# Key and value projections of six blocks of self attention: seven half-size products in place of eight, combined where they are stored

## Chip, cores and metric

The kernel runs on one core of one Trainium2 chip. The metric is device time in microseconds (us) of one execution. Before the change it is 2795.85 us, the median of 3 runs (2795.35 to 2799.18).

## What is computed

An encoder over a short context (2 x 77 tokens) and one decoder layer over 2 x 2048 tokens of width D = 512, 16 heads of 32, all in float32. The change concerns the keys and values of the decoder's causal self attention:

```python
yn = _ln(y, dec_n1_s, dec_n1_b)
wq, wk, wv = jnp.split(w_in, 3, axis=0)          # 512 x 512 each
bq, bk, bv = jnp.split(b_in, 3, axis=0)
q = yn @ wq.T + bq;  k = yn @ wk.T + bk;  v = yn @ wv.T + bv      # 16 heads of 32
scores = q k^T / sqrt(32) + bias            # relative bias, causal
attn = softmax(scores);  o = attn v
y = y + o @ w_out.T + b_out
```

After it come cross attention to the encoded context and a feed forward part of width 2048.

## The kernel before, in words

**Blocks, units and slots.** The tokens of each of the two sequences (b) are cut into 4 blocks (m) of MB = 512 tokens. A block is worked off in 16 units: 4 groups g of 4 heads times 4 tiles t of 128 queries, g outermost. So there are 128 units, numbered n; block x = 4b + m starts at unit u = 16x. A unit scores its queries against all keys up to its own, in pieces of up to four key tiles of 128, takes the exponential on ScalarE (ACT), turns the probabilities on TensorE (PE, line 425), copies them out of psum on ACT and VectorE (DVE; lines 429 and 431) and multiplies them by the values (line 442). The scores (line 374) of four heads run on four row groups of PE and go to four psum banks, which DVE empties with a running maximum (lines 383 and 390; line 400 closes the unit). Psum banks are handed out in rotation among 7.

**Slots.** Between the pieces of the units other work is put into numbered slots, one per unit, in an order written out by hand: `light[n]` first, then the `jobs[n]`, then `late[n]`; `ahead[n]` runs shortly before slot n. All engines have their instructions in this one program order, each engine goes through its own in order, and SyncE (SP) issues all loads and stores from one queue.

**Projections.** Each job of the list is a load and a run. `q_job` and `k_job` (lines 212 to 234) load 128 of the 512 output features (256 KB) into one of two `wqk` buffers and make one product of 4 accumulated matmuls of 128x128 weights by 512 tokens; a query tile is scaled on DVE (line 218), a key tile goes straight into `kT` with its bias, on DVE for m of 2 and 3 (line 230), else on ACT (line 232). `v_job` (lines 236 to 245) takes 128 tokens as the stationary operand and all of the 512x512 value weights as the moving one; they are loaded as 1 MB into `wbig` for each block, which `out_job` needs for the output weights in between. Line 243 adds the bias row `bv` on DVE into `vv`. A float32 matmul is two instructions on PE in the profile. A block of m = 1 to 3 has its key and value products in the slots -4 to 6 around its start u, one product to a slot or two. `load_next` keeps loads at most three jobs ahead and at most two of the `wqk` kind.

**Around it.** Slots also hold the layer norm of the next block (loads of x at slot +5 to +8 of the block before, statistics on DVE, centering on GpSimd (POOL, line 294), turning at PE line 306 and ACT line 311 one slot later), the reciprocal sums that go through DRAM (`rec` stores at line 463, `rirows` loads at line 468, four of each per group, and the product on POOL at line 470), the loads of the bias tables (line 342, four of 128 KB), and in the first 29 slots the encoder (weights of 1 MB each, line 521; its softmax steps on POOL at lines 594 and 606). In the blocks with m = 2, sums of weights for the feed forward part are made on POOL (line 1113, helper `minus`) and stored: that later part already uses seven half-size products for each eight, from line 1376 on. In the blocks of b = 1 the cross attention of the very first block is done beside self attention.

Of the kernel before, what the change touches and what calls it, by code (L numbers as in the profile page):

```python
# [12 lines left out]
ALU = mybir.AluOpType  # L13
# [41 lines left out]
def tile_encoder_decoder(ctx: ExitStack, tc: tile.TileContext, ins, out):  # L55
# [103 lines left out]
    with (  # L159
# [40 lines left out]
            nc.sync.dma_start(w, wchunk(name, c0, P))  # L200
            return w

        def big_w(kind, b, m):
            if wbig.get("is") != (kind, b, m):
                w = wbt
                nc.sync.dma_start(
                    w, wchunk("dec_sa_in_wT", 2 * D) if kind == "v" else wchunk("dec_sa_out_wT", 0)
                )
                wbig["is"], wbig["w"] = (kind, b, m), w
            return wbig["w"]  # L210

        def q_job(b, m, g):
            def run(w):
                mm = bank()
                for c in range(NC):
                    nc.tensor.matmul(mm, w[:, c, :], nTs[b, m][:, c, :], start=(c == 0), stop=(c == NC - 1))
# [19 lines left out]
        def v_job(b, m, t):  # L236
            def run(w):
                mm = bank()
                for c in range(NC):
                    nc.tensor.matmul(  # L240
                        mm, nTs[b, m][:, c, ts(t, P)], w[:, c, :], start=(c == 0), stop=(c == NC - 1)
                    )
                nc.vector.tensor_tensor(vv[:, m * TB + t, :], mm, bv, ALU.add)

            return lambda: big_w("v", b, m), run, False

        def out_job(b, m, t):
            def run(w):
                x1 = xr.pop((b, m, t))
                mm = bank()  # L250
                for c in range(NC):
                    nc.tensor.matmul(  # L252
                        mm, ots[b, m, c][:, ts(t, P)], w[:, c, :], start=(c == 0), stop=(c == NC - 1)
                    )
                nc.vector.tensor_tensor(x1, mm, x1, ALU.add)
                nc.sync.dma_start(y1[b][m][:, t, :], x1)

            return lambda: big_w("o", b, m), run, False

        def residual_load(b, m, t, place=None):  # L260
            x1 = sb.tile([P, D], F32, name="xr", tag="xr", bufs=2) if place is None else place
# [663 lines left out]
            return plan  # L925


        blocks = [(b, m) for b in range(B) for m in range(NMB)]
        NU = NC * TB
        jobs = {n: [] for n in range(-1, len(units) + NU)}  # L930
# [5 lines left out]
        for x, (b, m) in enumerate(blocks):  # L936
            u = x * NU
            first = m == 0

            jobs[max(u - 5 + (x == 1), -1)].append(q_job(b, m, 0))  # L940
            jobs[max(u - 4 + (x == 1), -1)].append(k_job(b, m, 0))
            jobs[(u + 1 if first else u - 3 + (x == 1)) if x else -1].append(v_job(b, m, 0))
            jobs[(u + 2 if first else u - 2 + (x == 1)) if x else 1].append(v_job(b, m, 1))
            jobs[u + 3 if first else u + 1].append(v_job(b, m, 2))
            jobs[u + 4 if first else u + 2].append(v_job(b, m, 3))
            jobs[u - 1 if x else 0].append(q_job(b, m, 1))
            jobs[u if x else 2].append(k_job(b, m, 1))
            for g, at, then in ((2, 3, 4), (3, 5, 6)) if x else ((2, 6, 7), (3, 8, 9)):
                jobs[u + at].append(q_job(b, m, g))
                jobs[u + then].append(k_job(b, m, g))  # L950
# [76 lines left out]
        light[-1].append(lambda: row_into(bo, "dec_sa_out_b"))  # L1027
        light[0].append(lambda: [self_bias(relg, vg, g) for g in range(1, NC)])
        light[1].append(lambda: make_bias(0, rel, v))
        light[6].append(lambda: make_bias(2, rel, v))  # L1030
        def slot(n):
            for f in light[n]:
# [59 lines left out]
        light[len(units) - 1].append(last_loads)  # L1092


        TOK = MB // 2
        gp, ve = nc.gpsimd, nc.vector


        w1_d = dram.tile([4, NC, P, D], F32, name="w1_d")
# [12 lines left out]
        def minus(engine, out, a, b):  # L1112
            engine.tensor_tensor(out, a, b, ALU.subtract)  # L1113

        def w2_sums(c):

# [49 lines left out]
        def quarter(name, r, c):  # L1166

            return ins[name][r * TOK : (r + 1) * TOK, c * TOK : (c + 1) * TOK].rearrange("(c p) o -> p c o", p=P)

        def wc_sums(name, turned):  # L1170
            z = free.rearrange("p (z k o) -> p z k o", z=8, k=2)
            q = {}
            for i, (r, c) in enumerate(((0, 0), (0, 1), (1, 0), (1, 1))):
                nc.sync.dma_start(z[:, i], quarter(name, c, r) if turned else quarter(name, r, c))
                q[r, c] = z[:, i]
            s1, s2, s3, s4 = (z[:, 4 + i] for i in range(4))
            if turned:
                gp.tensor_tensor(s1, q[1, 0], q[1, 1], ALU.add)
                minus(gp, s2, s1, q[0, 0])
                minus(gp, s3, q[0, 0], q[1, 0])  # L1180
                minus(gp, s4, q[0, 1], s2)
            else:
                minus(gp, s1, q[0, 1], q[0, 0])
                minus(gp, s3, q[1, 1], q[0, 1])
                minus(gp, s2, q[1, 1], s1)
                minus(gp, s4, q[1, 0], s2)

        def wc_store(dst):
            nc.sync.dma_start(
                dst.rearrange("s p x -> p s x"), free[:, 4 * D :].rearrange("p (s x) -> p s x", s=4)  # L1190
            )

        for u, name, turned, dst in (
            (2 * NU, "dec_ca_in_wT", True, wq_d), (6 * NU, "dec_ca_out_wT", False, wo_d)
        ):
            light[u + 7].append(lambda name=name, turned=turned: wc_sums(name, turned))
            late[u + 8].append(lambda dst=dst: wc_store(dst))
# [95 lines left out]
        def of_n(name):  # L1293
# [5 lines left out]
        T_OF = {"T1": ("12", "11"), "T2": ("22", "T1"), "T3": ("22", "12"), "T4": ("21", "T2")}  # L1299

        def sum_n(name, of):
            minus(gp, of(name), *(of(a) for a in T_OF[name]))


        sets = [[high[:, (4 * a + k) * D : (4 * a + k + 1) * D] for k in range(4)] for a in range(2)]
# [397 lines left out]
```

## Time and profile before

| | |
|---|---|
| median of 3 runs | 2795.85 us |
| profiled execution | 2796.27 us |
| its span, first to last instruction | 2794.2 us |
| mean granted clock of TensorE | 0.997 |
| self attention stage | about 0 to 1760 us of the span |
| DMA, mean over the span | 127 GB/s |

The page gives for each engine the time that it was busy, its share of the span and the number of instructions. PE is matmuls, PEld the loading of their weights, which overlaps. Groups of instructions are named by line and operation, with output <- input, shape and count, then busy time and mean ns of one, then the idle time of the engine just before them and what ended it. The timeline lists instructions in order, merged when alike: start, length, engine, line. Rows of waits give engine and line, what it waited for, the sum in us, how often, and the longest.

### The profile page before, as it was taken

The numbers are of one execution on the slowest core, as the hardware profiler recorded it, in microseconds if no ns is written. First come the engines' busy times: TensorE is split into PE (matmuls) and PEld (weight loads), VectorE is DVE, ScalarE is ACT, GpSimd is POOL, SyncE is SP. The second block draws the span as 40 slices with busy tenths as digits, with TensorE's granted clock in tenths as the row PEclk, the third lists the DMA queues.
The fourth block names the chain that finished last, engine by engine and source line by source line (L and its number), as shares of the span: only waits on it lengthen the run. The fifth ranks groups of instructions, "written<-read, shape, count | busy, mean of one in ns | idle before, by whom it ended". The sixth has DMA issues, their size and how long they took to land. (4 is left out here: it accounts for less than half of the span.)

```text
span 2794.2 us, 65938 instructions
## 1 busy us (share of the span) xinstructions
PE 2764.6 (99%) x25998; PEld 2076.6 (74%) x25998; DVE 1858.0 (66%) x5360; ACT 1435.3 (51%) x2751; POOL 875.6 (31%) x745
## 2 busy tenths in 40 slices
PE   9999999999999999999999999999999999999998
PEld 5567666666666556666666667898989898989898
DVE  5666587778887577687778885565555656464645
ACT  3544466656666556666646666434344444444431
POOL 0301143300100312122200001364747474746456
PEclk9999999999999999999999999999999999999999
DMA  6414344411112512232311014574747565656475
GB/s 194 116 56 135 111 143 123 139 31 48 38 41 73 140 47 70 84 107 92 106 33 39 26 50 134 174 242 145 237 152 236 175 226 163 223 162 220 148 226 181
DMA packets 281271, 355.31 MB, mean 127 GB/s; under 512 B 37968, under 2 KB 156544, under 8 KB 280834
## 3 DMA queue, kind: packets, MB, share of 16 engines
q1 hardware_dynamic: 280962, 351.10, 40.6%
q8 instruction: 206, 3.38, 0.5%
q14 instruction: 103, 0.84, 0.1%
HBM read 309.51 MB, written 41.49 MB: 126 GB/s over the span
## 5 line engine op out<-in xcount | busy, mean ns | idle before, releaser
L405 ACT ACTIVATE pp<-pp,nm 128x128 f32<-128x128 f32 (+15 forms) x512 | 612.0, 1203 | 137.2 <-DVE nm L400 136.8
L383 DVE TENSOR_SCALAR_CACHE_REDUCE pp<-psum 128x512 f32<-128x512 f32 (+3 forms) x1024 | 559.5, 591 | 64.0 <-PE psum L374 62.0
L431 ACT COPY pts<-psum 128x512 f32<-128x512 f32 (+3 forms) x592 | 300.5, 577 | 505.6 <-PE psum L425 369.7
L425 PEld LDWEIGHTS psum<-ident,pp 128*128 128x128 f32 x4352 | 473.1, 141 | 107.8 <-DVE pp L383 51.6
L425 PE MATMUL psum<-ident,pp 128*128 128x128 f32 x4352 | 533.6, 277 | 8.4 <-ACT pp L405 2.9
L429 DVE COPY pts<-psum 128x512 f32<-128x512 f32 (+2 forms) x544 | 330.0, 660 | 69.2 <-PE psum L425 67.7
L374 PE MATMUL psum<-kT,q 32*128 32x512 f32 (+3 forms) x2560 | 355.7, 576 | 5.2 <-DVE pp L383 2.6
L442 PEld LDWEIGHTS psum<-pts,vv 128*32 128x32 f32 x8704 | 225.6, 110 | 123.7 <-issue 115.8
L1405 PE MATMUL psum<-pp 128*128 128x128 f32 x2560 | 304.5, 276 | 1.9 <-POOL pp L1113 1.6
L1405 PEld LDWEIGHTS psum<-pp 128*128 128x128 f32 x2560 | 296.3, 192 | 8.6 <-issue 2.8
L442 PE MATMUL psum<-pts,vv 128*32 128x128 f32 x8704 | 278.2, 275 | 0.7 <-ACT pts L431 0.5
L1113 POOL TENSOR_TENSOR pp<-pp 128x512 f32<-128x512 f32 x159 | 212.5, 1353 | 111.1 <-DMA pp<-in_dec_ff_wT_dram 52.0
L1376 PE MATMUL psum<-vv,pp 128*128 128x256 f32 x1024 | 236.2, 381 | 0.0
L374 PEld LDWEIGHTS psum<-kT,q 32*128 32x128 f32 x2560 | 123.2, 183 | 140.7 <-issue 91.2
L1376 PEld LDWEIGHTS psum<-vv,pp 128*128 128x128 f32 x1024 | 190.3, 190 | 25.8 <-issue 0.5
L390 DVE CUSTOM_DVE_ANT_0 pp<-psum,bias 128x256 f32<-128x256 f32 (+1 forms) x512 | 196.0, 411 | 15.3 <-PE psum L374 15.2
L1389 DVE TENSOR_TENSOR kT<-kT,psum 128x512 f32<-128x512 f32 x96 | 65.8, 686 | 190.7 <-PE psum L1376 190.5
L1376 PE MATMUL psum<-nT,pp 128*128 128x256 f32 x768 | 174.1, 380 | 0.0
L1392 ACT ACTIVATE kT<-kT,vecs 128x256 f32<-128x256 f32 x192 | 87.0, 501 | 156.7 <-DVE kT L1389 156.0
L287 POOL TENSOR_TENSOR rstd<-rstd,mhalf 128x1 f32<-128x1 f32 x32 | 18.5, 578 | 458.7 <-DVE rstd L286 378.6
L1376 PEld LDWEIGHTS psum<-nT,pp 128*128 128x128 f32 x768 | 144.2, 190 | 20.3 <-issue 1.6
L470 POOL TENSOR_TENSOR oT<-rirows,oT 128x512 f32<-128x512 f32 x30 | 38.6, 1287 | 363.8 <-DMA rirows<-rec 187.8
(211 smaller groups left out, 3784.8 us busy)
## 6 DMA issues: line engine op xcount, KB each, us to landing
pp<-w_d SPq DMA_DIRECT2D x520, 256.0 KB
pp<-in_dec_ff_wT_dram SPq DMA_DIRECT2D x112, 256.0 KB
wqk<-in_dec_sa_in_wT_dram SPq DMA_DIRECT2D x64, 256.0 KB
bias<-tzg SPq DMA_DIRECT2D x128, 128.0 KB
pp<-wo_d SPq DMA_DIRECT2D x56, 256.0 KB
wbig<-in_dec_sa_in_wT_dram SPq DMA_DIRECT2D x8, 1024.0 KB
vv<-in_enc_ff_wT_dram SPq DMA_DIRECT2D x8, 1024.0 KB
xr<-in_x_dram SPq DMA_DIRECT2D x32, 256.0 KB
```

The lines of the kernel that those rows point to most:

```text
L374: nc.tensor.matmul(banks[r][:, : kn * P], q[rows4(r), ts(t, P)], kT[rows4(r), g, k0 * P : (k0 + kn) * P], start=True, stop=True,)
L383: nc.vector.tensor_scalar(p[:, k0 * P : (k0 + far) * P], s[:, : far * P], 1.0, None, ALU.mult, ALU.max, accum_out=st["mx"][:, r, c : c + 1],)
L390: nc.vector.tensor_tensor_reduce(p[:, (i + 1) * P - w : (i + 1) * P], s[:, far * P : kn * P], biases[b, m, g][:, r, 2 * P - w :], 1.0, LOW ...
L405: nc.scalar.activation(p, p, AF.Exp, bias=nm, accum_out=to)
L425: nc.tensor.transpose(pt[:, ts(x, P)], state[n]["p"][r][:, ts(k, P)], ident)
L429: nc.vector.tensor_copy(pts[:, : len(load), :], pt[:, :w])
L431: nc.scalar.copy(pts[:, : len(load), :], pt[:, :w])
L442: nc.tensor.matmul(ot[rows4(r), t, :], vv[:, k, ts(g * HC + r, HD)], got.pop((n, k, r)), start=(k == 0), stop=(k == i),)
L1113: engine.tensor_tensor(out, a, b, ALU.subtract)
L1376: nc.tensor.matmul(mm[:, ts(f, TOK)], a[:, c, ts(f, P)], b[:, c, :], start=fresh and f == 0 and c == 0, stop=c == 1, skip_group_check=True,)
L1392: nc.scalar.activation(dst[:, e, :], src[:, e, :], AF.Relu, bias=vec("dec_ff1_b", f + e))
L1405: nc.tensor.matmul(psum[:, bank_i, ts(col, P)], lhs[:, c, :], w[:, c, :], start=fresh and k in (0, 3) and c == 0, stop=c == 3, skip_group_ ...
```

## The change

For the six blocks with m of 1 to 3 the key and the value projection become seven products of half size each, by Strassen's scheme in Winograd's form. The weights (512 features in, 512 out) and the normalized tokens (512 features by 512 tokens) are both cut into quarters of 256x256. Four sums of weight quarters, S1 to S4, are made once for keys and once for values on POOL in the slots 2 and 5 (`wc_sums`, in a free part of `kT`) and kept in DRAM (`wc_store`, one slot later). Four sums of token quarters, T1 to T4, are made on POOL for each block five slots before it starts (`token_sums`), in the `xt` and `xr` buffers. Each product (`part_job`) loads 256 KB of weights into a `wqk` buffer, runs 2 x 2 matmuls with 256 columns into one psum bank, and is added on DVE into one or two quarters of `kT` or `vv`; the first one of seven is copied by ACT (keys with the bias of the first half of the features; `kstep`, the difference to that of the second half, is added with product 7).

The value bias is left out of `vv` in all blocks. Since the probabilities sum to one it can go to the output row: `fold_job` multiplies it by the output weights in slot 21 (one product of 512 columns, line 1048 of the changed program) and adds it to `bo`. The `wbig` buffer is reloaded only when its kind changes, no longer for each block. The order of products and slots, relative to u:

```diff
-            jobs[max(u - 5 + (x == 1), -1)].append(q_job(b, m, 0))
-            jobs[max(u - 4 + (x == 1), -1)].append(k_job(b, m, 0))
-            jobs[(u + 1 if first else u - 3 + (x == 1)) if x else -1].append(v_job(b, m, 0))
...
+            if first:
...
+            else:
+                (late if x == 1 else light)[u - 5].append(lambda b=b, m=m: token_sums(b, m))
+                todo = {
+                    -5: "q0", -4: "k1 k6", -3: "k7 k4", -2: "k2 k5", -1: "k3 v1", 0: "v6 v7", 1: "v4 v2", 2: "q1",
+                    3: "v5 v3", 4: "q2", 5: "q3",
+                } if x > 1 else {
+                    -4: "q0 k1", -3: "k6 k7", -2: "k4 k2", -1: "k5 k3", 0: "v1 v6", 1: "v7 v4 v2", 2: "q1",
+                    3: "v5 v3", 4: "q2", 5: "q3",
+                }
...
+            if x == 0:
+                jobs[NU + 5].append(fold_job())
```

Where the products go and what they are made of:

```diff
+        T_OF = {"T1": ("12", "11"), "T2": ("22", "T1"), "T3": ("22", "12"), "T4": ("21", "T2")}
+        PARTS = {
+            1: ("11", "11"), 2: ("12", "21"), 3: ("S4", "22"), 4: ("22", "T4"),
+            5: ("S1", "T1"), 6: ("S2", "T2"), 7: ("S3", "T3"),
+        }
+        ADDS = {2: ("11",), 3: ("12",), 5: ("22", "12")}
...
+            def run(w):
+                n, mm = of_nT(b, m, by), bank()
+                left, right = (w, n) if kind == "k" else (n, w)
+                for f in range(2):
+                    for c in range(2):
+                        nc.tensor.matmul(
+                            mm[:, ts(f, TOK)], left[:, c, ts(f, P)], right[:, c, :], start=c == 0, stop=c == 1,
+                        )
+                got = mm.rearrange("p (f n) -> p f n", f=2)
...
+                elif i == 6:
+                    ve.tensor_tensor(d["12"], got, d["11"], ALU.add)
...
+                else:
+                    for to in ADDS[i]:
+                        ve.tensor_tensor(d[to], got, d[to], ALU.add)
```

The rest of the diff in its core:

```diff
-            if wbig.get("is") != (kind, b, m):
+            if wbig.get("is") != kind:
...
-                nc.vector.tensor_tensor(vv[:, m * TB + t, :], mm, bv, ALU.add)
+                nc.vector.tensor_copy(vv[:, m * TB + t, :], mm)
...
-                row_into(bv, "sa_bv")
...
+        for n, kind in ((2, "k"), (5, "v")):
+            light[n].append(lambda kind=kind: wc_sums("dec_sa_in_wT", True, spare, sa_from[kind]))
+            late[n + 1].append(lambda kind=kind: wc_store(sa_d[kind], spare))
```

The helpers for such sums move up in the file from the feed forward part, and the store of four sums there becomes four stores.

More of the change, by code (lines that the diff above doesn't have):

```diff
@@ L208, in big_w @@
                 )
-                wbig["is"], wbig["w"] = (kind, b, m), w
+                wbig["is"], wbig["w"] = kind, w
             return wbig["w"]
@@ L925, in first_cross, with minus, sum_n, quarter @@
             return plan
+        TOK = MB // 2
+        gp, ve = nc.gpsimd, nc.vector
+        def minus(engine, out, a, b):
+            engine.tensor_tensor(out, a, b, ALU.subtract)
+        T_OF = {"T1": ("12", "11"), "T2": ("22", "T1"), "T3": ("22", "12"), "T4": ("21", "T2")}
+        def sum_n(name, of):
+            minus(gp, of(name), *(of(a) for a in T_OF[name]))
+        def quarter(name, r, c, c0=0):
+            o = c0 + c * TOK
+            return ins[name][r * TOK : (r + 1) * TOK, o : o + TOK].rearrange("(c p) o -> p c o", p=P)
@@ new lines, in wc_sums @@
+        def wc_sums(name, turned, z, c0=0):
+            z = [t.rearrange("p (k o) -> p k o", k=2) for t in z]
+            q = {}
+            for i, (r, c) in enumerate(((0, 0), (0, 1), (1, 0), (1, 1))):
+                nc.sync.dma_start(z[i], quarter(name, c, r, c0) if turned else quarter(name, r, c, c0))
+                q[r, c] = z[i]
+            s1, s2, s3, s4 = z[4:]
+            if turned:
+                gp.tensor_tensor(s1, q[1, 0], q[1, 1], ALU.add)
+                minus(gp, s2, s1, q[0, 0])
+                minus(gp, s3, q[0, 0], q[1, 0])
+                minus(gp, s4, q[0, 1], s2)
+            else:
+                minus(gp, s1, q[0, 1], q[0, 0])
+                minus(gp, s3, q[1, 1], q[0, 1])
+                minus(gp, s2, q[1, 1], s1)
+                minus(gp, s4, q[1, 0], s2)
@@ new lines, in wc_store @@
+        def wc_store(dst, z):
+            for i in range(4):
+                nc.sync.dma_start(dst[i], z[4 + i])
+        sa_d = {k: dram.tile([4, P, D], F32, name=f"sa_{k}", tag=f"sa_{k}") for k in "kv"}
+        sa_from = {"k": D, "v": 2 * D}
+        kstep = sm.tile([P, 2], F32, name="kstep", tag="kstep", bufs=1)
+        n_tiles = {}
+        PARTS = {
+            1: ("11", "11"), 2: ("12", "21"), 3: ("S4", "22"), 4: ("22", "T4"),
+            5: ("S1", "T1"), 6: ("S2", "T2"), 7: ("S3", "T3"),
+        }
@@ new lines, in part_job, with load, place @@
+        def part_job(kind, b, m, i):
+            name, by = PARTS[i]
+            def load():
+                w = sb.tile([P, NC, P], F32, name="wqk", tag="wqk", bufs=2).rearrange("p c o -> p (c o)")
+                w = w.rearrange("p (c o) -> p c o", c=2)
+                if name[0] == "S":
+                    src = sa_d[kind][int(name[1]) - 1].rearrange("p (c o) -> p c o", c=2)
+                else:
+                    src = quarter("dec_sa_in_wT", int(name[1]) - 1, int(name[0]) - 1, sa_from[kind])
+                nc.sync.dma_start(w, src)
+                return w
+            def place(to):
+                r, c = int(to[0]) - 1, int(to[1]) - 1
+                if kind == "k":
+                    return kT[:, 2 * r : 2 * r + 2, m * MB + c * TOK : m * MB + (c + 1) * TOK]
+                return vv[:, m * TB + 2 * c : m * TB + 2 * c + 2, ts(r, TOK)]
+            def run(w):
[7 more added lines that the diff above has]
+                got = mm.rearrange("p (f n) -> p f n", f=2)
+                d = {to: place(to) for to in ("11", "12", "21", "22")}
+                if i == 1 and kind == "k":
+                    for f in range(2):
+                        nc.scalar.activation(
+                            d["11"][:, f, :], got[:, f, :], AF.Identity, bias=vec("dec_sa_in_b", NC + f)
+                        )
+                elif i == 1:
+                    nc.scalar.copy(d["11"], got)
+                elif i == 6:
+                    ve.tensor_tensor(d["12"], got, d["11"], ALU.add)
+                elif i == 7 and kind == "k":
+                    for f in range(2):
+                        ve.scalar_tensor_tensor(
+                            d["22"][:, f, :], got[:, f, :], kstep[:, f : f + 1], d["12"][:, f, :], ALU.add, ALU.add
+                        )
+                elif i == 7:
+                    ve.tensor_tensor(d["22"], got, d["12"], ALU.add)
+                elif i == 4:
+                    ve.tensor_tensor(d["21"], got, d["22"], ALU.add)
+                else:
+                    for to in ADDS[i]:
+                        ve.tensor_tensor(d[to], got, d[to], ALU.add)
+            return load, run, True
@@ L928, in tile_encoder_decoder, with fold_job, run @@
+        def fold_job():
+            def run(w):
+                mm = bank()
+                for c in range(NC):
+                    nc.tensor.matmul(
+                        mm, vec("dec_sa_in_b", 2 * NC + c).to_broadcast([P, P]), w[:, c, :],
+                        start=(c == 0), stop=(c == NC - 1),
+                    )
+                ve.tensor_tensor(bo, mm, bo, ALU.add)
+            return lambda: big_w("o"), run, False
         blocks = [(b, m) for b in range(B) for m in range(NMB)]
@@ L1029, in tile_encoder_decoder @@
         light[1].append(lambda: make_bias(0, rel, v))
+        light[1].append(
+            lambda: minus(ve, kstep, *(vecs[:, o : o + 2] for o in (_COL["dec_sa_in_b"] + NC + 2, _COL["dec_sa_in_b"] + NC)))
+        )
+        spare = [kT[:, g, (2 + h) * MB : (3 + h) * MB] for g in range(NC) for h in range(2)]
+        for n, kind in ((2, "k"), (5, "v")):
+            light[n].append(lambda kind=kind: wc_sums("dec_sa_in_wT", True, spare, sa_from[kind]))
+            late[n + 1].append(lambda kind=kind: wc_store(sa_d[kind], spare))
         light[6].append(lambda: make_bias(2, rel, v))
@@ L1092, in tile_encoder_decoder @@
         light[len(units) - 1].append(last_loads)
-        TOK = MB // 2
-        gp, ve = nc.gpsimd, nc.vector
         w1_d = dram.tile([4, NC, P, D], F32, name="w1_d")
@@ L1110, in tile_encoder_decoder @@
         SUBS = ("11", "21", "T2", "T1", "T3", "22", "T4")
-        def minus(engine, out, a, b):
-            engine.tensor_tensor(out, a, b, ALU.subtract)
         def w2_sums(c):
@@ L1164, in w1_store @@
             )
[L1166 to L1191, printed above, removed]
         for u, name, turned, dst in (
@@ L1195, in tile_encoder_decoder @@
         ):
-            light[u + 7].append(lambda name=name, turned=turned: wc_sums(name, turned))
-            late[u + 8].append(lambda dst=dst: wc_store(dst))
+            z = free.rearrange("p (z x) -> p z x", z=8)
+            z = [z[:, i] for i in range(8)]
+            light[u + 7].append(lambda name=name, turned=turned, z=z: wc_sums(name, turned, z))
+            late[u + 8].append(lambda dst=dst, z=z: wc_store(dst, z))
         u = 2 * NU
```

42 lines of the change are left out of this document (28 added, 14 removed).

## The prediction

> **What bounds the kernel now.** I read first the page's busy shares and the 40 slices, then the windows of the self attention stage, then the PE timeline inside one unit.
>
> ```profile
> span 2794.2 us, 65938 instructions
> PE 2764.6 (99%) x25998; PEld 2076.6 (74%) x25998; DVE 1858.0 (66%) x5360; ACT 1435.3 (51%) x2751; POOL 875.6 (31%) x745
> ```
>
> ```profile
> 80.00:160.00 80.00, 73.22 (x587) 41.61 (x584) 50.16 (x192) 39.08 (x113) 24.13 (x17) 0.96 0.28 72
> 640.00:780.00 140.00, 139.93 (x1705) 95.28 (x1702) 118.84 (x370) 90.93 (x135) 16.74 (x13) 1.00 0.16 48
> 1500.00:1600.00 100.00, 99.97 (x1231) 68.07 (x1224) 82.03 (x250) 62.80 (x88) 5.09 (x4) 1.00 0.12 38
> ```
>
> The window columns are length, PE, PEld, DVE, ACT, POOL, clock, DMA share, GB/s. PE has no idle time in the deep blocks (139.93 of 140), while DVE is at 82 to 85%. A busy PE can hide stalls, so I took the pitch, start to start, from the timeline; the last two rows are of the feed forward stage, whose products have the new shape:
>
> ```profile
> 1469.85 3.60 PE L240 MATMUL psum<-wbig,nT 128*128 128x512 f32 x8
> 1473.38 1.14 PE L374 MATMUL psum<-kT,q 32*128 32x512 f32 x8
> ...
> 1870.21 7.07 PE L1376 MATMUL psum<-nT,pp 128*128 128x256 f32 x32
> 1877.12 0.60 PE L781 MATMUL psum<-ident,q 128*128 128x128 f32 x4
> ```
>
> A value product (8 instructions of 512 columns) takes 1473.38 - 1469.85 = 3.53 us of PE; 32 instructions of 256 take 6.91, so 8 take 1.73. The engine runs such groups end to end. PE's own work is the bound, except around 100 to 121 us and where its weights wait for DVE:
>
> ```profile
> PEld psum L425 <- DVE pp L383: 51.6, 83, 1.5
> ```
>
> That is 51.6 us in 83 waits, none over 1.5.
>
> **The change, part by part.** Times go against the profiled execution, 2796.27 us (span 2794.2 and 2.07 around it), 0.4 above the median of 2795.85.
>
> *PE.* In each of six blocks 4 key and 4 value products go: 8 x 3.53 = 28.2 us. 14 half-size ones come: 14 x 1.73 = 24.2. What 3.53 has over 2 x 1.73, 0.07, I read as the change to the row-tiled scores; it is paid in 7 slots, 0.5 to 0.7 in all. Saving 28.2 - 24.2 - 0.6 = 3.4 per block, 20.4 in six. fold_job adds one product of 512 columns, 3.53. Net **-16.9 us** of PE work.
>
> *DVE and ACT.* The rows that go and the nearest of those that come:
>
> ```profile
> L243 DVE TENSOR_TENSOR vv<-psum,row_sa_bv 128x512 f32<-128x512 f32 x32 | 22.1, 692 | 59.9 <-PE psum L240 59.9
> L230 DVE TENSOR_SCALAR kT<-psum,vecs 128x512 f32<-128x512 f32 x14 | 10.5, 750 | 17.1 <-PE psum L227 17.1
> L232 ACT ACTIVATE kT<-psum,vecs 128x512 f32<-128x512 f32 x16 | 10.9, 684 | 28.9 <-PE psum L227 28.8
> L390 DVE CUSTOM_DVE_ANT_0 pp<-psum,bias 128x256 f32<-128x256 f32 x432 | 169.8, 419 | 12.7 <-PE psum L374 12.7
> ```
>
> Per block 13 adds of 128x512 into the destination come (6 for keys, 7 for values) and two of 128x256: 13 x 0.692 + 2 x 0.42 = 9.8 us. Four value adds go (2.8), and four key evictions, on DVE for m of 2 and 3 (3.0), on ACT for m = 1. DVE gains 4.0 in four blocks and 7.0 in two: 30 us. ACT gains three copies of about half a microsecond per block and loses 2.7 where m = 1. If DVE were the bound this would cost 30 us; it idles 15 to 18% in the tightest windows, some 20 us per 140, so its share rises by a few per cent. What matters is the queue: behind a part's add stand the score evictions that free psum banks. Before, one add of 0.69 to 0.75 stood there; now the first part's add ends during the second part's 1.73 us of PE, so only the second part's counts, 0.69, except after k5 (two adds, 1.38). One slot per block, 0.7 later: 0 to 4 us in all, I take 0.5, since the slot's values products lie in between.
>
> *POOL.* 4 sums per block and 8 for the weights:
>
> ```profile
> L1113 POOL TENSOR_TENSOR pp<-pp 128x512 f32<-128x512 f32 x35 | 44.0, 1275 | 52.8 <-DMA pp<-in_dec_ff_wT_dram 52.0
> ```
>
> 32 x 1.275 = 41 us on an engine that is busy 31%. The sums of a block are issued five slots ahead; T2 is first used one slot later, 6.6 us at the least (below), after 2 x 1.275. Hidden; without that cover it would cost up to 2.6 us a block.
>
> *Weight loads.* This is the new wait. Two wqk buffers serve 14 parts instead of 4 key products, so the load for a slot's second part is issued only when the previous slot's second part has left PE, and stands on SP's queue behind what is there. The loads of wbig for values and output fall from 16 to 4, which frees SP. A landing, bounded:
>
> ```profile
> 474.97 1.97 SPq L1174 DMA_DIRECT2D pp<-in_dec_ca_in_wT_dram  x4
> 481.54 1.28 POOL L1178 TENSOR_TENSOR pp<-pp 128x512 f32<-128x512 f32 x1 [0.59 <-DMA pp<-in_dec_ca_in_wT_dram]
> ```
>
> Four 256 KB loads are in 4.6 us after the last issue and 6.6 after the first; one alone I estimate at 2.5 to 3 (a quarter of 6.6 is 1.6 as the lower end, 4.6 the upper). By the Trainium skill, page "DMA: Bandwidth & Descriptors", section "Anatomy of one DMA — SWDGE (gpsimd) path", a transfer costs some 2.0 us plus its bytes at 436 GB/s, so an estimate of 2.6 us here; no row shows it alone. A slot that lasts longer than the way of SP and the landing hides that. The shortest slots of any of the six blocks:
>
> ```profile
> 979.35 3.60 PE L216 MATMUL psum<-nT,wqk 128*128 128x512 f32 x8
> ...
> 987.06 3.70 PE L227 MATMUL psum<-nT,wqk 128*128 128x512 f32 x8
> ...
> 993.63 3.70 PE L240 MATMUL psum<-wbig,nT 128*128 128x512 f32 x8
> ```
>
> ```profile
> 987.24 2.70 SPq L463 DMA_DIRECT2D rec<-rt  x4
> 989.98 1.87 SPq L342 DMA_DIRECT2D bias<-tzg  x4
> 991.96 0.40 SPq L200 DMA_DIRECT2D wqk<-in_dec_sa_in_wT_dram  x1
> ```
>
> In the sixth block (b = 1, m = 1) the slots start at 979.4, 987.1 and 993.6. k1 leaves PE at 988.8, then SP issues k7's load, four rec stores (2.7) and four bias loads (1.9), and k4's load at about 993.7, landing at 996.2 to 997. k4 follows k7, so PE wants it at 995.4: **+1.5** (0 to 3). In the second block it is worse, because the slot with "v7 v4 v2" has three parts, and SP is held by an encoder row:
>
> ```profile
> 166.84 0.32 SPq L526 DMA_DIRECT2D pp<-in_rows_dram  x1
> ...
> 171.95 0.39 SPq L200 DMA_DIRECT2D wqk<-in_dec_sa_in_wT_dram  x1
> ```
>
> ```profile
> 170.08 3.60 PE L240 MATMUL psum<-wbig,nT 128*128 128x512 f32 x8
> ```
>
> v4's load stands behind that row, rec and bias, so it is issued at about 172 and lands at 175 (the 512 KB of bias go ahead); v7 begins at 170.1 and is done at 171.8. v2's load is issued after v7 and lands with the end of v4. **+3.4** (0 to 7). The w2 loads and stores of the third block, which ran ahead of their slots on SP, now wait for the slots too, with q3's weights behind them; I take nothing for it, up to 5 us if q3 is late.
>
> *The first 120 us.* 2 MB more are loaded and stored for the sums, and the value sums stand on POOL ahead of this chain:
>
> ```profile
> 81.04 2.25 POOL L594 TENSOR_TENSOR pp<-pp,emx 77x1232 f32<-77x1232 f32 x1 [2.64 <-DMA rirows<-rec]
> ...
> 104.14 1.28 POOL L470 TENSOR_TENSOR oT<-rirows,oT 128x512 f32<-128x512 f32 x1
> ```
>
> ```profile
> 110.46 1.67 PE L306 MATMUL psum<-ident,xr 128*128 128x128 f32 x8
> ```
>
> POOL is nearly full from 81 to 105. Sums of 5.1 us that begin when their loads land (I estimate 78) delay it by 3 to 8; the centered rows are wanted by PE at 110.5, so most is covered. I take **+1.5** (0 to 8).
>
> Sum: 2796.3 - 16.9 + 0.5 + 1.5 + 3.4 + 1.5 = 2786.3; against the median, **2786 us**.
>
> **The rivals.**
>
> *The loads are late in every short slot.* For: two buffers and an SP that issues one load in 0.4 us and eight others ahead of it in 4.6. Against: in most slots nothing stands between, and 6.6 us is over a landing of 3. If each of the 7 part slots of the second and the sixth block waits 1 us more, 14 us come on top: **2800**; half of that gives 2793. The saving is gone, no more.
>
> *A slower kernel: the value sums hold POOL in the encoder.* They stand in front of the centering of the second block's rows and both softmax steps. If their loads, queued behind the encoder's 1 MB weights, land at 95 instead of 78, the chain ends some 20 us later, at 125, and PE waits for the rows of 110.5 for about 15; the token sums and k6 come late behind it. The clock adds to this:
>
> ```profile
> 100.00:121.00 21.00, 17.33 (x142) 12.79 (x141) 12.12 (x54) 14.32 (x41) 5.42 (x3) 0.84 0.27 83
> ```
>
> Here PE already idles 3.7 of 21 us and its clock is 0.84, so 0.16 x 21 = 3.4 us are lost to it; a longer wait would lose as much again. 2786 + 15 + 3 = **2804**. It decides from a start of the value sums after about 92 us. The Trainium skill, page "TensorE: Matmul & The Clock Gate", section "Why this matters for your kernels", warns of PE gaps over some 3 us for the same reason; the trace agrees with 0.84.
>
> *Half-size products are not half the time.* If weights did not load beside the matmul:
>
> ```profile
> L1376 PE MATMUL psum<-vv,pp 128*128 128x256 f32 x1024 | 236.2, 381 | 0.0
> L1376 PEld LDWEIGHTS psum<-vv,pp 128*128 128x128 f32 x1024 | 190.3, 190 | 25.8 <-issue 0.5
> ```
>
> each of the 112 instructions would cost 190 + 216 ns against 64 of 190 + 441: 45.5 - 40.4 = 5 us more per block, 30 in six, **2837** with the fold and the waits. Against it: the same rows give 6.91 us for 32, with no idle. The Trainium skill, same page, section "Back-to-back issue gap", has sustained spacings of 81 ns at 128 columns and 131 at 512, by which halving the columns would save far less than half; the pitches of 3.53 and 1.73 contradict it here.
>
> *Better than forecast.* The loads land in time and the half-clock windows shrink: 2796 - 17 - 1 = **2778**.
>
> **How the numbers follow.** Chances: forecast (2783 to 2790) 0.50, better (below 2783) 0.12, late loads (2790 to 2801) 0.24, slower through POOL and clock (above 2801) 0.12, half-size products 0.02. A measurement of this kernel tells 0.2%, 5.6 us, from no change. Faster (below 2790.3) has 0.62, the same 0.24, slower 0.14. The range leaves out the half-size case, most of the slower one and the extreme of the better one: 2779 to 2800.
>
> **What would show it.** Right: PE starts of two parts in a slot 1.73 apart; waits of PE for wqk by DMA of 1 to 4 us in two slots, one about 995 and one about 172, and none over 0.5 elsewhere; DVE share of 640 to 780 up by 2 to 4 points with the waits on L383 still near 52 us; POOL's value sums before 85 us. Wrong: PE waits for DMA in a dozen slots (late loads); PE idle between 100 and 130 us well above the present 7 (POOL); pitch over 1.8 (half-size); waits on L383 over 65 us (DVE as the bound).

## The result, and the profile after

The changed kernel takes 2820.7 us (median of 5 runs, 2818.72 to 2821.75) against 2796.77 (5 runs, 2795.35 to 2799.18) for the kernel before: a ratio of 1.0083, 95% interval 1.0072 to 1.0095. It is 24 us slower, where the forecast was 2786 (2779 to 2800). The profiled execution has a span of 2819.2 us, 25.0 more than before. Of the kernels below, the one with all edits and the one with the early sums alone each had one execution far out (7026 and 3477 us), which their medians leave out.

The first two lines of the page of after, to be read against the two at the top of the prediction:

```profile
span 2819.2 us, 66842 instructions
PE 2771.8 (98%) x26294; PEld 2146.2 (76%) x26294; DVE 1886.7 (67%) x5412; ACT 1440.2 (51%) x2761; POOL 915.1 (32%) x777
```

PE's busy time was to fall by 16.9 us and rose by 7.2; its idle time (span less busy) rose from 29.6 to 47.4. Yet the pitch is the forecast one. The timeline of after on PE, in a slot with two parts in the third block (the next one's start less one's own):

```profile
567.22 1.89 PE L1014 MATMUL psum<-nT,wqk 128*128 128x256 f32 x8
568.95 1.89 PE L1014 MATMUL psum<-xt,wqk 128*128 128x256 f32 x8
570.77 0.71 PE L374 MATMUL psum<-kT,q 32*128 32x256 f32 x8
```

The parts take 1.73 and 1.82. So work did leave PE, and something else came. Three views say what. First, PE's waits in after for the weights, of which before had one, of 0.5 us:

```profile
PE psum L1014 <- DMA wqk<-in_dec_sa_in_wT_dram: 8.1, 4, 5.0
PE psum L1014 <- DMA wqk<-sa_k: 7.5, 2, 6.2
PE psum L216 <- DMA wqk<-in_dec_sa_in_wT_dram: 1.6, 1, 1.6
```

17.2 us in 7 waits. That is nearly all of the added idle time, and two of the waits, 4.99 (slot 17) and 6.20 (slot 94), make two thirds of it; of the others the longest are 1.74 (at 357 us, the step of unit 30 below) and 1.64 (at 93 us).

Second, the clock. The records of the granted clock show it at half, apart from the program's last microseconds, in three stretches of before and in seven of after. In the windows, PEclk is the third column from the end:

```profile
110.70:114.10 3.40, 3.40 (x24) 3.30 (x22) 1.82 (x4) 3.40 (x11) 0.00 (x0) 0.50 0.02 5
117.50:120.90 3.40, 3.40 (x26) 3.07 (x19) 0.90 (x4) 0.76 (x2) 0.00 (x0) 0.50 0.00 0
1462.40:1469.20 6.80, 6.80 (x28) 4.98 (x26) 5.91 (x23) 1.35 (x3) 0.00 (x0) 0.50 0.01 2
```

```profile
178.20:185.00 6.80, 3.85 (x9) 3.17 (x10) 0.06 (x1) 0.03 (x1) 0.00 (x0) 0.50 0.36 111
482.00:485.40 3.40, 3.40 (x17) 3.31 (x18) 2.38 (x15) 2.12 (x5) 2.94 (x2) 0.50 0.02 5
642.40:649.20 6.80, 6.80 (x28) 4.98 (x25) 5.26 (x19) 1.99 (x4) 0.00 (x0) 0.50 0.01 2
1212.40:1219.20 6.80, 5.48 (x16) 3.04 (x16) 1.29 (x2) 0.00 (x0) 0.00 (x0) 0.50 0.25 81
1331.90:1335.30 3.40, 3.40 (x18) 3.40 (x17) 1.75 (x11) 2.46 (x5) 2.29 (x2) 0.50 0.00 0
1492.30:1499.10 6.80, 6.80 (x27) 4.85 (x25) 5.24 (x17) 2.41 (x4) 0.00 (x0) 0.50 0.00 0
113.30:123.50 10.20, 9.31 (x66) 7.92 (x65) 3.87 (x15) 6.30 (x18) 5.00 (x4) 0.50 0.01 2
```

PE worked 13.6 us at half clock before and 39.0 after; at half rate half of it is lost, so 6.8 against 19.5: some 13 us more. Of these, 4.7 lie at the two long waits (the windows at 178 and 1212), 3.4 in the slots u+6 of the blocks with m = 2 (482 and 1332), 3.4 near 640 and 1.3 in the first 125 us.

Third, where the saving should appear. With two parts in a slot (3.5 us) in place of one product, a slot's PE work hardly changes; what a block saves is one whole product, the one of slot u+6, which has k3 before and nothing after. DVE closes each unit at line 400, so the delay of after against before can be read unit by unit (start of that instruction in both traces, us):

```
unit    0    9   12   15   16   17   18   22   23   30   37   39   40   50   55   79   87   94   95  103  104  114  119  127
delay 0.7  2.5  2.9  6.3  2.9  4.2 13.5 17.0 15.6 17.5 17.7 16.8 18.5 20.8 18.6 20.4 17.8 18.6 27.7 26.8 28.7 29.4 26.3 25.2
```

The steps that cost are at units 9 (1.8), 18 (9.3, with 1.7 for the third part of slot 17), 30 (1.9), 40 (1.7), 50 (2.3), 95 (9.1) and 104 (1.9); the fold's 3.4 at 22 is as forecast. The bare slots u+6 gave back 1.4 (unit 23), 0.9 (39), 2.2 (55), 2.5 (87), 1.0 (103) and 3.1 (119): 11.1 us, not 20.4.

So the balance on PE against the forecast work of -16.9 us is: 17.8 more idle time, 13 lost to the clock, and 9.3 of the saving that didn't come because the slot it was taken from didn't get that much shorter. -16.9 + 17.8 + 13 + 9.3 = 23; 2 of the 25.0 are in none of these, and the terms, which are read separately, may overlap a little.

**The two long waits.** In slot 94, two ahead of the seventh block, the timeline of after has, on SP and on PE:

```profile
1208.95 0.58 SPq L921 DMA_DIRECT2D nT_d<-pp  x1
1209.63 0.56 SPq L922 DMA_DIRECT2D y<-pp  x1
1210.28 1.00 SPq L1000 DMA_DIRECT2D wqk<-sa_k  x2
```

```profile
1205.63 1.89 PE L1014 MATMUL psum<-nT,wqk 128*128 128x256 f32 x8
1213.72 3.75 PE L1014 MATMUL psum<-xt,wqk 128*128 128x256 f32 x8 [6.20 <-DMA wqk<-sa_k]
```

The weights of the slot's second part are issued at 1210.28, when its first part has been done for almost 3 us (1205.63 + 1.89), because two stores of the first cross attention stand ahead of them and SP waited 9.6 us for ACT to fill what they store:

```profile
SPq L921 <- ACT pp L784: 9.6, 1, 9.6
```

The same wait stands in the trace of before, 13.6 us long, with a weight load behind it; nothing came late there, since each of these slots needed one load, which was in already:

```profile
SPq L921 <- ACT pp L784: 13.6, 1, 13.6
```

In slot 17 the queue is the one that the prediction described (timeline of after, SP), with both loads behind it instead of one; the product of the first of them is on PE in the last row:

```profile
172.78 0.32 SPq L526 DMA_DIRECT2D pp<-in_rows_dram  x1
173.15 2.67 SPq L463 DMA_DIRECT2D rec<-rt  x4
175.86 1.87 SPq L342 DMA_DIRECT2D bias<-tzg  x4
177.83 0.91 SPq L1000 DMA_DIRECT2D wqk<-in_dec_sa_in_wT_dram  x2
```

```profile
181.15 3.75 PE L1014 MATMUL psum<-wqk,xr 128*128 128x256 f32 x8 [4.99 <-DMA wqk<-in_dec_sa_in_wT_dram]
```

**The bare slot.** Slot 38 (u = 32, m = 2) in the windows of before and of after. PE's, PEld's and DVE's busy time follow the length:

```profile
456.80:467.50 10.70, 10.70 (x74) 6.02 (x69) 10.22 (x39) 8.23 (x13) 3.89 (x3) 1.00 0.41 122
```

```profile
474.50:484.30 9.80, 9.05 (x56) 5.32 (x51) 9.49 (x38) 7.50 (x11) 3.25 (x3) 0.88 0.03 10
```

In this slot DVE is busy 10.22 of 10.70 us: it empties three score pieces of four banks in a row. I read it as the bound here, with PE's product beside it; two of the experiments below test that. Without the product the slot is 0.9 shorter. In the timeline of PE, before:

```profile
459.90 3.60 PE L227 MATMUL psum<-nT,wqk 128*128 128x512 f32 x8
463.43 1.14 PE L374 MATMUL psum<-kT,q 32*128 32x512 f32 x8
```

and after:

```profile
477.71 2.71 PE L374 MATMUL psum<-kT,q 32*128 32x512 f32 x8
480.35 0.42 PE L442 MATMUL psum<-pts,vv 128*32 128x128 f32 x8
481.52 0.42 PE L442 MATMUL psum<-pts,vv 128*32 128x128 f32 x8 [0.74 <-DVE pts L429]
```

The same scores take 2.71 instead of 1.14, which I read as waits for banks, and then comes the half-clock window at 482.0. PE's "busy" hides most of this wait: only 0.74 of it is a row.

### The profile page after: what moved, and what is told of

Its sections match the earlier page's. It is cut to its first block, busy times and chain, and to the rows that moved or that the text cites. A ratio compares the mean times of both kernels' runs of the same rounds, so it can differ in the third digit from the quotient of the medians.

```text
span 2819.2 us, 66842 instructions
## 1 busy us (share of the span) xinstructions
PE 2771.8 (98%) x26294; PEld 2146.2 (76%) x26294; DVE 1886.7 (67%) x5412; ACT 1440.2 (51%) x2761; POOL 915.1 (32%) x777
## 5 line engine op out<-in xcount | busy, mean ns | idle before, releaser
L425 PEld LDWEIGHTS psum<-ident,pp 128*128 128x128 f32 x4352 | 478.2, 142 | 110.9 <-DVE pp L383 53.7
L425 PE MATMUL psum<-ident,pp 128*128 128x128 f32 x4352 | 540.2, 279 | 9.4 <-ACT pp L405 3.3
L374 PE MATMUL psum<-kT,q 32*128 32x512 f32 (+3 forms) x2560 | 365.5, 578 | 4.9 <-DVE pp L383 2.9
L1526 ACT COPY oT<-psum 128x128 f32<-128x128 f32 x56 | 15.0, 267 | 239.0 <-PE psum L1518 239.0
```

Source lines behind the costliest of these rows:

```text
L374: nc.tensor.matmul(banks[r][:, : kn * P], q[rows4(r), ts(t, P)], kT[rows4(r), g, k0 * P : (k0 + kn) * P], start=True, stop=True,)
L425: nc.tensor.transpose(pt[:, ts(x, P)], state[n]["p"][r][:, ts(k, P)], ident)
```

## The experiments

Theory 1 is that weights come late; theory 2 that the product that left the slots u+6 had been cover for DVE, and that its absence costs both the saving and the clock. All ratios are to the kernel before.

**A third weight buffer.** `w_tile` gives every third load the row tile `bv`, which nobody uses until the first cross attention is through.

```diff
-            w = sb.tile([P, NC, P], F32, name="wqk", tag="wqk", bufs=2)
+            w = w_tile()
...
-            while len(loaded) < min(len(queue), ran[0] + (5 if ran[0] < 4 else 3)):
+            while len(loaded) < min(len(queue), ran[0] + (5 if ran[0] < 4 else 4)):
...
-                if sum(ahead) > 2:
+                if sum(ahead) > 3:
```

> The kernel after, with a third buffer for the small weights (the row tile that nobody uses until the first cross attention is through) and each load issued one product earlier. Theory 1 (late weights): the PE waits for weights, 17.2 us in 7 waits of after, go to under 2 us, and the half-clock windows that follow the two longest of them (6.8 us each, at half rate some 3.4 us lost in each) go with them: 2820.7 - 16 - 7 = 2798, like the kernel before. Theory 2 (what is lost is cover: the product taken out of the sixth slot of the late blocks, and the clock): the waits go too, but PE then waits for DVE in the same slots, and the time comes down by less than 8: 2813 or above.

Measured: 2799.86 us, ratio 1.0009 (1.0001 to 1.0018), 20.8 less than after. One wait for weights is left, in slot 17:

```profile
PE psum L1020 <- DMA row_sa_bv<-in_dec_sa_in_wT_dram: 3.3, 1, 3.3
```

Slot 94 costs 0.1 instead of 9.1. Theory 2 as the whole story is refuted. Not all of the 20.8 belongs to the weights: by units, 4.2 of it come where after has the half-clock windows of 1332 and 1492 and this kernel has none. And without late weights the kernel is still only level with before, so the saving is missing elsewhere.

**q3 into the slot u+6, in the two blocks with m = 2.**

```diff
+                if m == 2:
+                    todo[6] = todo.pop(5)
```

> The kernel after, with the last q product of the two blocks with m = 2 one slot later (six slots behind the block's start instead of five), so that this slot holds a product of 3.4 us beside its scores again, as in the kernel before. The work is the same. Theory 2 (lost cover): in slots 38 and 102 the PE waits for DVE (some 3 us) and the half-clock window behind them (3.4 us in the first, 1.7 to 3.4 lost) go: 5 to 10 us faster over both, 2811 to 2816. Theory 1: a slot's product more or less changes nothing but where the weights are loaded; within 2 us of 2820.7.

Measured: 2809.82 us, ratio 1.0046 (1.0033 to 1.0058), 10.9 less than after with the same work, a little more than expected. Now the slots 37 and 101 are bare. There the scores run freely; timeline of PE in this kernel, slot 37:

```profile
464.31 1.14 PE L374 MATMUL psum<-kT,q 32*128 32x512 f32 x8
```

The bare slots give 3.5 and 3.4 us here, the whole product, and the half-clock windows at 482 and 1332 are gone. By units, these slots and the ones behind them are worth 8.6; another 4.8 come because the windows near 640 and 1492 are absent too, which the edit doesn't explain, and 2.1 are lost before unit 37. So which slot loses its product decides, but not all of the 10.9 is due to it.

**The kernel before, with k3 of these blocks one slot earlier.**

```diff
-            for g, at, then in ((2, 3, 4), (3, 5, 6)) if x else ((2, 6, 7), (3, 8, 9)):
+            for g, at, then in ((2, 3, 4), (3, 5, 5 if m == 2 else 6)) if x else ((2, 6, 7), (3, 8, 9)):
```

> The kernel before, with the last k product of the two blocks with m = 2 put one slot earlier (in the slot of q3), nothing else changed: the same work with slots 38 and 102 bare. Theory 2: these slots lose their cover as in after, PE waits for DVE and the clock falls behind it: 3 to 8 us slower, 2800 to 2805. Theory 1: no weights are late (they are loaded in the same order, one slot earlier is enough), the time stays at 2797 within 1.5.

Measured: 2805.67 us, ratio 1.0031 (1.002 to 1.0043): 8.7 slower without any of the change's products. Slot 38 shows the same picture as in after:

```profile
463.37 2.71 PE L374 MATMUL psum<-kT,q 32*128 32x512 f32 x8
...
467.18 0.43 PE L442 MATMUL psum<-pts,vv 128*32 128x128 f32 x8 [0.74 <-DVE pts L429]
```

By units, slot 37 grows by 3.5 and slot 38 gives back 1.0, twice (2.5 each); 2.0 more comes at unit 50 from a half-clock window at 626, and the span is 6.8 longer in all. The median is a little above the expected range. One part of theory 2 fails here: the clock stays at full in both bare slots. The window of slot 38 in this kernel:

```profile
460.20:470.20 10.00, 9.26 (x66) 5.41 (x61) 9.58 (x39) 8.26 (x13) 3.49 (x3) 1.00 0.01 2
```

So the lost saving is DVE's doing (9.58 of 10.00 us) and not the clock's; and the fall of the clock doesn't follow from the bare slot alone.

**Both edits in one kernel**, the first diff and the second.

> The kernel after with both edits: the third weight buffer, and the last q product of the two blocks with m = 2 one slot later. If both theories hold in their sizes, 2820.7 - 23 - 7 = 2791, faster than the kernel before by some 6. If theory 1 alone holds: 2798. If neither: above 2810.

Measured: 2790.32 us, ratio 0.9977 (0.9967 to 0.9987). The two gains, 20.8 and 10.9, nearly add up: 30.4. Both theories hold, each for its part.

**Loads issued right behind each product, two buffers.**

```diff
                 run(loaded[ran[0]])
                 ran[0] += 1
+                load_next()
```

> The kernel after with one more call that issues the next weight load right behind each product, still with two buffers: a load then stands in SP's order ahead of what the slot issues at its end and at the next slot's start, instead of behind it. Nothing else is changed. If the weights were late because of their place in SP's order (the stores of the first cross attention in slot 94, the bias and row loads in slot 17), the PE waits for weights fall from 17.2 to under 5 us and the time by as much as the third buffer gave: 2800. If two buffers are too few whatever the order (a load can't be issued before the buffer's last reader is done), it changes by less than 5: 2816 or above.

Measured: 2800.45 us, ratio 1.0012 (1.0003 to 1.0021), as good as the third buffer. In the timelines of SP and PE the load for the second part of slot 94 is now issued at 1190.01, ahead of the stores, which wait for ACT as before, and the two parts run 1.73 apart:

```profile
1190.01 0.34 SPq L1000 DMA_DIRECT2D wqk<-sa_k  x1
...
1199.69 0.58 SPq L921 DMA_DIRECT2D nT_d<-pp  x1
```

```profile
1196.37 1.89 PE L1014 MATMUL psum<-nT,wqk 128*128 128x256 f32 x8
1198.10 1.89 PE L1014 MATMUL psum<-xt,wqk 128*128 128x256 f32 x8
```

So two buffers suffice in slot 94; what made the weights late there is where their loads stand in SP's order. One wait, 3.8 us in slot 17, stays. This kernel has the later half-clock windows of after (at 474, 634, 1313 and 1474), so it is the cleaner measure of the late weights: its span is 18.5 us shorter, the clock behind the waits included.

**Idle work in the bare slots of after.**

```diff
+        for n in (2 * NU + 6, 6 * NU + 6):
+            late[n].append(lambda: warm(16))
```

> The kernel after with 16 idle transposes of 128x128 (some 3.4 us of TensorE, nobody reads them) added in each of slots 38 and 102, where the kernel before had the product. The work grows by 6.9 us. If the slots are set by DVE and the pause costs clock (theory 2), the added work lies in time that PE waits anyway and the half-clock windows at 482.0 and 1331.9 go: no slower than 2820.7, down to 2815. If work on TensorE is what counts: 2827.

Measured: 2814.69 us, ratio 1.0066 (1.0052 to 1.008): 6.0 faster than after, with more work. The transposes took some 1.9 us in each slot, not 3.4 as I had put it, so 3.8 us were added. Timeline of PE:

```profile
477.50 1.91 PE L1147 MATMUL psum<-ident 128*128 128x128 f32 x16
479.34 1.58 PE L374 MATMUL psum<-kT,q 32*128 32x512 f32 x8
...
481.76 3.93 PE L425 MATMUL psum<-ident,pp 128*128 128x128 f32 x32
```

Line 425 begins at 481.76, in after at 481.88: the added work took no time. And its 32 instructions take 3.93 us where they took 5.38, most of it at half clock. Both half-clock windows are gone. That work on TensorE in itself is what counts is refuted for these slots. The 6.0 is not their price: the profiled execution (2811.43) is the fastest of the five, 9.6 under after's span, and by units 3.2 of that come in and behind the two slots, 4.7 from the windows near 640 and 1492, absent here as well, and 1.3 from slot 94.

**Loads behind each product, q3 in u+6 in all six blocks, two buffers:** the diff of the loads, and the second diff without its `if`.

> The kernel after with the loads issued right behind each product and q3 one slot later in all six blocks, two buffers. If order is the cause of the late weights: 2800, less 11 for the two blocks with m = 2 as measured, less some 3 for the other four blocks (they got 1.4 to 3.1 of the 3.4 us each): 2786. If it isn't: 2807.

Measured: 2788.26 us, ratio 0.997 (0.9958 to 0.9981). Two lines of edits, with the change's products as they are, turn 24 us lost into 9 won.

**The same with the third buffer** of the first diff.

> The kernel with the third buffer and q3 late in all six blocks, and loads issued right behind each product. From 2790.3 (third buffer, q3 late in two blocks): less up to 5 for the stall that is left in slot 17 (3.2 us and its half-clock window) and less 3 for q3 in the other four blocks: 2782 to 2786. If the order of the loads gives nothing with three buffers: 2787 to 2790.

Measured: 2785.4 us, ratio 0.9956 (0.9942 to 0.9969), 35 less than after. It is the best median of all, though its interval overlaps with the preceding one's. PE waits for no weights any more. Its page:

```profile
PE 2753.8 (99%) x26294; PEld 2136.2 (77%) x26294; DVE 1885.9 (68%) x5412; ACT 1439.1 (52%) x2761; POOL 915.2 (33%) x777
```

PE's busy time is 10.8 under before's, where 16.9 had been forecast.

**The early sums alone, on the kernel before.** The eight loads, sums and stores of weight combinations in the slots 2 to 6 are added; nobody reads what they make.

```diff
+        for n, kind in ((2, "k"), (5, "v")):
+            light[n].append(lambda kind=kind: sa_sums({"k": D, "v": 2 * D}[kind]))
+            late[n + 1].append(lambda kind=kind: sa_store(sa_d[kind]))
```

> The kernel before, plus only the early preparation: the eight quarter loads, the eight sums on POOL and the stores of the combinations of the key and value weights in slots 2 to 6, in the same places as in after. Nobody reads them, and the projections stay as they are. As predicted: 1.5 us for them, within 2796 to 2800. If the start of after is late because of them (2.9 us by the thirteenth unit), it shows here by then, as a wait of a product for its weights near 93 us; if it is the order of the first block's own loads, the time stays at 2797.

Measured: 2800.5 us, ratio 1.0013 (1.0005 to 1.0022): 3.3 us for the preparation, a little more than the expected range. In the trace 4.0 come between the ends of units 8 and 9, where q3's weights are late and the clock is at half from 93.4 on (3.4 us), so that the product takes 5.37 instead of 3.6:

```profile
91.98 5.37 PE L216 MATMUL psum<-nT,wqk 128*128 128x512 f32 x8 [2.14 <-DMA wqk<-in_dec_sa_in_wT_dram]
```

## Why the prediction was wrong

**The failed step is the weight loads, and beside it the PE term.** The sum has +4.9 us for late weights (1.5 and 3.4); with the clock behind them they cost some 18.5. It has -20.4 for the products that go, as if PE were the bound in every slot that loses one; 9.3 of that didn't come: 5.0 in the two slots of the blocks with m = 2, where DVE was the bound, and the rest in the other four, which were not taken apart. Point by point:

- *Pitch of the parts, the fold:* right. 1.73 apart, the fold 3.4 (forecast 3.53). The half-size rival is out.
- *Weight loads:* wrong in size and place. The two slots named were late, but slot 17 cost 9.3, of which 1.7 is its third part, and not 3.4 more than that part, for both loads stood behind the queue and the clock fell with it (the first, issued at 177.83, let PE go on at 181.15, 3.3 us later, where the estimate of a landing was 2.5 to 3); the slot near 995 (at 1015 in after) cost 1.1 of 1.5. Slot 94 was missed. The step searched for the *shortest* slots; late weights come where SP is *held longest*, and the 9.6 us wait for ACT's slab could be read beforehand as 13.6 in before's own waits of SP. "In most slots nothing stands between" was true, and still two slots made 16.7 us (7.6 and 9.1).
- *PE, "the bound":* wrong for the slots that mattered. The 140-us window's 82 to 85% for DVE is a mean; in slot 38 DVE has 10.22 of 10.70. Of 20.4 saved, 11.1 arrived. A bare slot 37 gives up 3.4 to 3.5 us where a bare slot 38 gives 0.9 to 1.0: 2.5 us per block, which the second and third experiments show from either side.
- *The clock:* taken into account for 100 to 121 us only. Some 13 us more were lost to it in all, 8.1 of them at the long waits and in the bare slots. "The trace agrees with 0.84" says too much: between 100 and 121 no gap of PE in before is over 1.41 us, and the clock is at half from 110.7 all the same.
- *The first 120 us:* 1.5 against 3.3 measured alone and 2.9 in after by unit 12 (0.7 of it there at unit 0). The path was another one. POOL's value sums were early enough, at 78 to 83 us (the first two rows below). But their four stores hold SP until 88.7, 5 us after the sums are done, and q3's weights stand behind: issued at 89.31 in after, at 80.78 in before. The profile puts the longest wait of these stores, 3.7 us, to the landing of an encoder weight. In the timelines of after and of before, with that wait on SP between them:

```profile
78.17 1.27 POOL L952 TENSOR_TENSOR kT<-kT 128x512 f32<-128x512 f32 x1 [22.81 <-DMA kT<-in_dec_sa_in_wT_dram]
79.52 3.74 POOL L932 TENSOR_TENSOR kT<-kT 128x512 f32<-128x512 f32 x3
...
82.12 6.62 SPq L964 DMA_DIRECT2D sa_v<-kT  x4
...
89.31 0.71 SPq L200 DMA_DIRECT2D wqk<-in_dec_sa_in_wT_dram  x1
```

```profile
SPq L964 <- DMA vv<-in_enc_ff_wT_dram: 3.7, 1, 3.7
```

```profile
80.78 3.88 SPq L200 DMA_DIRECT2D wqk<-in_dec_sa_in_wT_dram  x1
```

- *DVE's queue:* right as a mean. DVE's busy time over the span rose by 28.7 us (forecast 30). The waits for line 383 are 53.7 us in 87 (forecast "near 52"), and DVE's share of 640 to 780 rises from 118.84 to 120.02 of 140, 0.8 points where 2 to 4 were expected (the same stretch of time holds work that comes some 20 us earlier in before):

```profile
PEld psum L425 <- DVE pp L383: 53.7, 87, 1.5
640.00:780.00 140.00, 139.69 (x1636) 97.55 (x1636) 120.02 (x379) 90.20 (x128) 14.13 (x11) 0.98 0.12 36
```

- *The rivals:* "late in every short slot" has the right cause but the wrong shape (few and long); its end, that the saving is gone and no more, left out the clock and the lost cover. "Value sums hold POOL" is out: sums at 78, before its point of 92. The measured time lies in the band that had been set aside for it (above 2801), but by another mechanism.

The Trainium skill, page "TensorE: Matmul & The Clock Gate", section "Why this matters for your kernels", names gaps over some 3 us; the windows at 178.2 and 1212.4, at waits of 4.99 and 6.20, agree, and those behind shorter gaps show that it isn't the whole rule. Its section "A second HAM failure mode: psum-queue depth-cycling" tells of a bf16 kernel whose clock falls from frequent short idling between groups of matmuls; slot 38 of after, in float32, agrees, with one counted gap of 0.74 us, and with idle transposes in the slot the clock stayed up. The same slot with the same gap kept the full clock in the kernel before with k3 early.

**What parts the windows that come from those that don't.** The half-clock windows of 6.8 us near 630 to 640 and near 1470 to 1490 come in some of these kernels and not in others (the first in after, with the third buffer, with k3 early, with both edits, with the loads behind each product and in the best kernel; the second in before, in after, with k3 early and with the loads behind each product). PE's gaps ahead of them are the same with and without, 1.2 and 0.3 us. The clock records allow a reading. In each trace the starts of the half-clock windows lie whole multiples of 3.413 us apart (in after 19 times from 113.34 to 178.19, 404 times from 113.34 to 1492.32), so I cut each trace into cells of this length. As the work of a cell I count, for each matmul instruction, 0.861 ns per column (3.53 us over 8 x 512; twice that at half clock), times the share of the array's rows and columns that it uses: a quarter for a score of 32 rows. From 20 to 1780 us the eleven profiles have 5601 cells at full clock. In 40 of them the work is 0.36 of the cell or less, and the clock is at half in the next cell each time; of 14 between 0.36 and 0.40 this is so for 6, of the 5547 above for none. The lowest cell of slot 38 has 0.33 in after and 0.50 with k3 early; near 640 it has 0.31 in after and 0.45 with q3 in u+6, near 1490 0.39 and 0.44. So where a slow stretch of about a cell's length falls on this raster seems to decide, and everything ahead of it shifts that. It is an estimate from one profile of each kernel; no run was made to test it.

By unit 18 even the best kernel is 3.9 us behind before; that remainder was not taken apart beyond the early sums and stays open.

## What to carry to other kernels

A product that leaves the tensor engine is worth its length only in a slot where PE is the bound: take the windows slot by slot before choosing which one goes bare, and leave bare one in which the engine that empties psum has slack. When more, smaller loads replace few large ones, read the load queue's own waits in the profile before: each long wait of the queue is a place where the second load of a slot will be late. A pause of PE must be priced with the clock behind it, and a stretch in which PE is busy but waits inside its instructions can cost clock as well.

## What the hardware showed that I had not expected

The granted clock fell to half in a slot in which PE showed only 0.74 us of waiting on a semaphore and 0.75 us of idle time in 9.8 (windows 482.0 and 1331.9 of after). With some 1.9 us of idle transposes in these slots, nothing else changed, it stayed at full. Of the eight bare slots of this kind in the profiles (after, third buffer, loads behind each product, k3 early; two each) five have such a window; of the fourteen of the other seven kernels, which have a product or transposes in the slot, none has. Except for the one that runs into the end of the program, half-clock stretches came as 3.4, 6.8 and 10.2 us in all kernels, and on a raster of 3.413 us.
